# A 5x5 convolution as four 64x64 matmul tiles side by side for eight channels, with its four middle rows on VectorE

## The chip, the cores and the metric

The kernel runs on one NeuronCore of a Trainium2 chip. The metric is the device time of one execution in microseconds, as the median of the runs. In the profile PE is TensorE's matmul, PEld its weight load, DVE is VectorE, ACT is ScalarE, POOL is GpSimd, which also issues most DMAs, and SP is SyncE, which issues the others.

## What is computed

The input is 8 images of 32 channels of 128x128, in float32. Two layers are applied, each of the form x + conv(groupnorm(x)), where the group norm works on groups of two channels.

Layer 0's `conv` is a block-matching filter: for each pixel the eight best of 25 shifted copies are picked by 3x3 patch distance and gathered, and the 256 planes then go through three 1x1 convolutions, each followed by a depthwise 3x3, a product with a DCT of the planes, and an aggregation back to 32 channels. Layer 1's `conv`, which the change is about, is one 5x5 kernel, the same for every channel, with zero padding of 2:

```python
x = x + _L0_conv_ref(_gn(x), ...)
# layer 1: kernel is (5, 5), one for all channels
Xf = X.reshape(B * C, 1, H, W)
out = lax.conv_general_dilated(Xf, kernel[None, None, :, :],
                               window_strides=(1, 1), padding=[(2, 2), (2, 2)], ...)
x = x + out.reshape(B, C, H, W)     # X is _gn(x)
```

## The kernel before

**Steps.** Layer 0 of an image is cut into 17 strips, so there are 8 x 17 = 136 steps (image b, n = 0 to 16), each with four sub-steps i = 3, 2, 1, 0 for the three stages of 1x1 and depthwise convolution and the gathering. The stages lag one another by a step. A step ends, for its strip, with the DCT products (L757 on PE, L760 on DVE) and the aggregation (`pa`, L773 on PE), which is added to the input strip, put into the running statistics and stored to the DRAM buffer `x1d` (L785). For half of the planes the depthwise taps run on DVE as chains of eight `scalar_tensor_tensor` (L688, opened by ACT at L685 and closed by ACT at L692), for the other half on PE in four column tiles of 32 (L709).

**Order.** The orders of PE, DVE and ACT are written out by hand: they are the order of the Python program (`manual_schedule`). The orders of POOL and SP, and with them the DMA queues, are laid out by the framework's scheduler. Side work is written as generators that wait in four queues, "D", "A", "P" and "Q", each item with a cost. At every sub-step `tick` grants the "D" queue a credit, a share of `total`, and the items that fit are emitted there; the other queues are emptied once a sub-step. Side work is `prep(b + 1)`, the patch distances of the next image (differences on DVE at L410, squares on ACT at L418, sums on PE at L425, stores `sq` at L440, window sums on DVE at L474 to L486, sources for the gathering through `xl` and `xtd` at L383 to L395), and `layer1(b)`.

**Layer 1.** `layer1(b)` is pushed when strip 16 of image b has been aggregated. It forms mean and inverse deviation per channel, spreads them to all partitions as `bc` (ACT copy, L806), and then works on four channels at a time, with an image row on each of the 128 partitions: load `xy` from `x1d` (L812), four normalisations of 128x128 into `xm` on DVE (L817), five matmuls of a 128x128 band matrix, one for each dx, into one PSUM bank (L836), the addition to `xy` (L847), and the store (L848). Two `xy` tiles are used in turn, so the load for channels c + 8 follows the store of channels c:

```python
yield "D", 2.1
if c + 4 < C:
    xm = normalise(c + 4)
xy = xys.pop(c)
nc.vector.tensor_add(xy, xy, ps)
nc.gpsimd.dma_start(out[b, c : c + 4].rearrange("c y x -> y c x"), xy)
load(c + 8)
```

The matrix `band[:, dx]` holds the five taps of column dx on its diagonals; it is built once, at the start, on DVE (L329). For images 0 to 6, layer 1 runs as side work in the first steps of the next image; after the last image it runs alone (`until`).

A load of `final_load` for the next strip (`xf`, L744) reads the DRAM buffer `xbd` that the gathering has stored (L608).

Of the kernel before, what the change touches and what calls it, by code (L numbers as in the profile page):

```python
# [9 lines left out]
F32 = mybir.dt.float32  # L10
# [3 lines left out]
ALU = mybir.AluOpType  # L14
ORDERED = {mybir.EngineType.PE, mybir.EngineType.DVE, mybir.EngineType.Activation}

P = 128
C, K, H, W = 32, 8, 128, 128
# [7 lines left out]
HR = 38  # L26
HX = W + 4
SR = 6
# [15 lines left out]
def bm3d_conv_preact(  # L44
# [16 lines left out]
    nc = tc.nc  # L61
    NB = x.shape[0]
# [3 lines left out]
    xnp = ctx.enter_context(tc.tile_pool(name="xn", bufs=1))  # L66
    work = ctx.enter_context(tc.tile_pool(name="work", bufs=2))
# [3 lines left out]
    ps_x = ctx.enter_context(  # L71
        tc.tile_pool(name="ps_x", bufs=5, space=bass.MemoryType.PSUM)
    )
# [49 lines left out]
    band = const.tile([P, 5, P], F32, name="band")  # L123
    kb = const.tile([P, 25], F32, name="kb")
# [22 lines left out]
    with tc.tile_pool(name="setup", bufs=1) as sp, tc.tile_pool(  # L147
        name="setup_ps", bufs=2, space=bass.MemoryType.PSUM
# [22 lines left out]
        for name, w in (("w1", w1), ("w3", w3), ("w5", w5)):  # L171
            t = sp.tile([P, 2, CK], F32, name=f"nat_{name}", tag=f"nat_{name}")
            nc.sync.dma_start(t, w.rearrange("(m p) i a b -> p m (i a b)", p=P))
            if name == "w1":

                nat, t = t, sp.tile([P, 2, CK], F32, name="w1_kc")
# [6 lines left out]
        for name, dst in (("w1", lw1), ("w3", lw3), ("w5", lw5)):  # L183
            for g in range(2):
                ps = spp.tile([P, CK], F32, name=f"ps_{name}_{g}", tag="ps")
                for m in range(2):
                    src = wide[name][:, m, g * P : (g + 1) * P]
# [15 lines left out]
    xtd, xbd, idxd, x1d, stats = {}, {}, {}, {}, {}  # L203
# [12 lines left out]
    def push(task):  # L216
        want = next(task, None)
        if want:
            which, cost, *wait = want
            queues[which].append((cost, task, now[0] + (wait[0] if wait else 0)))  # L220
# [568 lines left out]
    def layer1(b):  # L789

        yield "D", 0.2
        mv = work.tile([P, 2], F32, name=f"mv1_{b}", tag="mv1")
        nc.vector.bn_aggr(mv, stats[b].rearrange("p a b -> p (a b)"))
        mr = yield from group_stats(mv, f"b{b}")
        dg = work.tile([C, 2, C], F32, name=f"dg_{b}", tag="dg")
        for i in range(2):
            nc.vector.tensor_scalar(
                dg[:, i], ident[:C, :C], mr[:C, i : i + 1], None, op0=ALU.mult
            )
        yield "P", 0  # L800
        pb = ps_x.tile([P, 512], F32, name=f"pb_{b}", tag="x")
        nc.tensor.matmul(
            pb[:, : 2 * C], ones, dg.rearrange("p a b -> p (a b)"), start=True, stop=True
        )
        bc = work.tile([P, 2, C], F32, name=f"bc_{b}", tag="bc")
        nc.scalar.copy(bc.rearrange("p a b -> p (a b)"), pb[:, : 2 * C])  # L806
        xys = {}

        def load(c):
            if c < C:  # L810
                xys[c] = work.tile([P, 4, W], F32, name=f"xy_{b}_{c}", tag="xy")
                nc.gpsimd.dma_start(xys[c], x1d[b][c : c + 4].rearrange("c y x -> y c x"))  # L812

        def normalise(c):
            xm = work.tile([P, 4, W], F32, name=f"xm_{b}_{c}", tag="xm")
            for i in range(4):
                nc.vector.tensor_scalar(  # L817
                    xm[:, i],
                    xys[c][:, i],
                    bc[:, 0, c + i : c + i + 1],  # L820
                    bc[:, 1, c + i : c + i + 1],
                    op0=ALU.subtract,
                    op1=ALU.mult,
                )
            return xm

        load(0)
        load(4)
        yield "D", 1.4
        xm = normalise(0)  # L830
        for c in range(0, C, 4):
            yield "P", 0
            ps = ps_x.tile([P, 4, W], F32, name=f"p5_{b}_{c}", tag="x")
            for n, dx in enumerate((0, -2, -1, 1, 2)):
                xa, xz = max(0, -dx), min(W, W - dx)
                nc.tensor.matmul(  # L836
                    ps[:, :, xa:xz],
                    band[:, dx + 2],
                    xm[:, :, xa + dx : xz + dx],
                    start=n == 0,  # L840
                    stop=n == 4,
                )
            yield "D", 2.1
            if c + 4 < C:
                xm = normalise(c + 4)
            xy = xys.pop(c)
            nc.vector.tensor_add(xy, xy, ps)  # L847
            nc.gpsimd.dma_start(out[b, c : c + 4].rearrange("c y x -> y c x"), xy)  # L848
            load(c + 8)

        done.add(b)

    done = set()

# [12 lines left out]
    def unit(stage, u):  # L867
        if 0 <= u < len(units) and units[u]:
            if stage is gather_load:
                at = (units[u][0], units[u][1] % 8 // 2)  # L870
                until(lambda: at in ready, 4.0)
            stage(*units[u])
# [7 lines left out]
        if n == NS:  # L880
            push(layer1(b))

    total = 5.5 + 3.3 + 36 * 1.95 + 4 * 4.6 + 32 * 1.85 + 4 * 2.6 + 8 * 2.1
    owed = [0.0]

    def tick(b, i):
# [6 lines left out]
    def until(cond, credit):  # L893
        while not cond():
            now[0] += 1
            run("D", credit)
            run("A")
            run("P")
            run("Q")

    with tc.manual_schedule(engines=ORDERED):
        push(prep(0))
        push(mixes())
        xbd[0] = dram.tile([P, 2, H, W], F32, name="xbd_0", tag="xbd")
        for i in range(3):
            nc.gpsimd.memset(tb[i][0:64, :, 0], 0.0)
        for u in range(7):
            unit(gather_load, u)
            unit(gather_select, u - 2)
            unit(gather_pixels, u - 3)  # L910
        u = 4

        dt = dv = kept = iter(())

        later = lambda: None

        for s in range(len(steps) + 2):
            if s < len(steps):
                b, n = steps[s]
                if s == 2:  # L920
                    push(bands())
                if n == (0 if b else 4) and b + 1 < NB:
                    until(lambda: b in ready, 4.0)
                    push(prep(b + 1))
                if n == NS - 1 and b + 1 < NB:
                    until(lambda: b + 1 in ready, 4.0)
                    xbd[b + 1] = dram.tile([P, 2, H, W], F32, name=f"xbd_{b+1}", tag="xbd")
            for i in (3, 2, 1, 0):
                si = s - (i - 1 if i else 2)
                live = 0 <= si < len(steps)  # L930
                new_v = new_t = iter(())
                if live:
                    bi, ni = steps[si]

                if live and i:
                    src = source(i, bi, ni)
                    pointwise_v(i, bi, ni, lws[i - 1], src)
                    new_v, new_t = depthwise_v(i, bi, ni), depthwise_t(i, bi, ni)
                    accs[i, bi, ni] = [None, next(new_v)]
                later()  # L940
                later = lambda: None
                if live and not i:
                    if ni == 0:
                        x1d[bi] = dram.tile([C, H, W], F32, name=f"x1d_{bi}", tag="x1d")
                        stats[bi] = work.tile([P, NS + 1, 6], F32, name=f"stat_{bi}", tag="stat")
                    xr, xf, j0, j1 = fins.pop(si)
                run("P")
                if live and not i:
                    final_dct(bi, ni, accs[3, bi, ni], xf, j0, j1)

                run("Q")
                if s < len(steps):
                    unit(gather_select, u + 1)
                    unit(gather_load, u + 3)
                    tick(b, i)
                next(new_v, None)
                if live and i:
                    pointwise_t(i, bi, ni, lws[i - 1], src)
                next(kept, None)
                if not i:  # L960
                    next(dt, None)
                if s < len(steps):
                    unit(gather_pixels, u)
                    u += 1
                if i:
                    next(dt, None)
                run("A")
                next(dv, None)
                next(dt, None)
                kept, dv, dt = dv, new_v, new_t  # L970
                if live and not i:
                    later = partial(end, bi, ni, xr, j0, j1)
                if not i and 0 <= s - 1 < len(steps):
                    fins[s - 1] = final_load(*steps[s - 1])
        next(kept, None)
        later()
        until(lambda: NB - 1 in done, 4.0)


# [60 lines left out]
```

## Time and profile before

| | |
|---|---|
| median of 3 runs | 7144.41 us (7131.88 to 7159.89) |
| the profiled execution | 7131.18 us, its span 7129.4 us |
| granted TensorE clock, mean | 0.978 |
| PE busy | 6700.9 us, 94% of the span, 100226 instructions |
| DVE busy | 5840.1 us, 82% |
| ACT busy | 5061.7 us, 71% |
| POOL busy | 2738.3 us, 38% |
| 5x5 matmuls (L836) | 294.3 us of PE, 640 instructions |
| normalisations (L817) | 74.6 us of DVE, 256 instructions |
| additions (L847) | 43.7 us of DVE, 64 instructions |
| loads (L812), stores (L848) | 49.8 and 50.9 us of POOL, 64 each |

Busy time is summed over the whole span; the span holds 136 steps and the layer 1 of the last image, which begins at about 7056 us and runs with little beside it. One `matmul` of the program is two instructions in the profile here: five matmuls on four channels are ten.

### The profile page before, as it was taken

To read this page: it belongs to the slowest core of one execution; us is meant where nothing else is said; L and a number is where in the kernel's file an instruction comes from. 1 tells how busy PE (TensorE), PEld (TensorE's weight loads), DVE (VectorE), ACT (ScalarE), POOL (GpSimd) and SP (SyncE) were. 2 spreads that over 40 slices of the span, in tenths; PEclk is the share of its full clock that TensorE was granted. 3 is DMA by queue.
4 is the path that set the end of the run, shared out by engine and by line. 5 is a ranking of instruction groups with operands and counts; after the bars stand their busy time and mean duration, and the time that the engine had idled before them with its cause. 6 is when DMAs were issued, how large, how long until landed. Compare 5 with 4: busy or idle time off the path is not lost. (4 is left out here: it accounts for less than half of the span.)

```text
span 7129.4 us, 229485 instructions
## 1 busy us (share of the span) xinstructions
PE 6700.9 (94%) x100226; PEld 3166.8 (44%) x100226; DVE 5840.1 (82%) x8606; ACT 5061.7 (71%) x6706; POOL 2738.3 (38%) x4599
## 2 busy tenths in 40 slices
PE   4699999999999999999999999999999999999997
PEld 1344444444444444444444444444444444444443
DVE  6689978888888898878888898888978889767675
ACT  4687768677686777867677776877768677666762
POOL 6244336333353343533335343543335333232222
PEclk8899999999999999999999999999999999999999
DMA  3566756666565575666656666566656666555652
GB/s 81 130 145 151 155 129 153 142 148 149 134 156 143 138 166 125 160 145 145 154 127 160 141 152 140 142 161 150 152 130 150 151 145 147 125 146 139 149 134 63
DMA packets 765484, 1007.70 MB, mean 141 GB/s; under 512 B 215008, under 2 KB 578592, under 8 KB 764480
## 3 DMA queue, kind: packets, MB, share of 16 engines
q0 software_dynamic: 378400, 733.67, 42.5%
q1 hardware_dynamic: 381056, 256.86, 17.0%
q8 instruction: 788, 12.91, 0.8%
q10 hardware_dynamic: 5024, 2.49, 0.2%
q14 instruction: 216, 1.77, 0.1%
HBM read 542.24 MB, written 217.01 MB: 106 GB/s over the span
## 5 line engine op out<-in xcount | busy, mean ns | idle before, releaser
L688 DVE SCALAR_TENSOR_TENSOR acc<-tv,dwv,acc 128x1024 f32<-128x1024 f32 (+1 forms) x3264 | 4084.0, 1253 | 223.1 <-ACT acc L685 109.5
L709 PE MATMUL pw<-t,dwd 128*32 128x508 f32 (+6 forms) x19584 | 2179.5, 592 | 156.8 <-DMA t<-t 109.4
L709 PEld LDWEIGHTS pw<-t,dwd 128*32 128x32 f32 (+1 forms) x19584 | 702.3, 111 | 1393.8 <-issue 1205.9
L570 POOL DMA_DIRECT2D ib<-idxd x1024 | 575.2, 563 | 1881.5 <-ACT sel L585 1764.8
L584 ACT ACTIVATE ib<-ib,nplace 128x1024 bf16<-128x1024 bf16 x1024 | 1165.4, 1138 | 25.6 <-DMA ib<-idxd 25.6
L585 ACT ACTIVATE sel<-ib 128x1024 f32<-128x1024 bf16 x1024 | 1084.4, 1059 | 32.6
L660 PE MATMUL p<-acc,lw 128*32 128x256 f32 x17408 | 994.1, 375 | 10.3 <-issue 10.0
L637 PE MATMUL pv<-acc,lw 128*128 128x512 f32 (+1 forms) x2112 | 971.9, 602 | 10.5 <-DVE acc L760 6.3
L606 ACT COPY xb<-pg 128x512 f32<-128x512 f32 x512 | 303.6, 593 | 713.5 <-PE pg L599 713.1
L645 ACT COPY tv<-pv 128x512 f32<-128x512 f32 (+2 forms) x784 | 444.8, 584 | 482.0 <-PE pv L637 463.6
L660 PEld LDWEIGHTS p<-acc,lw 128*32 128x32 f32 x17408 | 562.8, 110 | 429.6 <-issue 81.0
L721 ACT ACTIVATE acc<-pw 128x512 f32<-128x512 f32 (+1 forms) x816 | 452.8, 584 | 341.2 <-PE pw L709 340.8
L599 PEld LDWEIGHTS pg<-sel,xt 128*32 128x32 f32 x45056 | 591.2, 111 | 225.7 <-issue 126.1
L599 PE MATMUL pg<-sel,xt 128*32 128x48 f32 x45056 | 593.6, 206 | 82.9 <-issue 53.1
L780 DVE TENSOR_TENSOR xr<-xr,pa 128x256 f32<-128x256 f32 (+2 forms) x136 | 55.1, 405 | 717.9 <-PE pa L773 698.8
L637 PEld LDWEIGHTS pv<-acc,lw 128*128 128x128 f32 x2112 | 381.0, 191 | 407.7 <-issue 376.7
L410 DVE TENSOR_TENSOR df<-xn 128x786 f32<-128x786 f32 (+2 forms) x576 | 529.0, 969 | 17.2 <-PE pd L425 14.6
L667 ACT COPY t<-p 128x512 f32<-128x512 f32 x800 | 423.0, 570 | 119.8 <-PE p L660 116.5
L418 ACT ACTIVATE df<-df 128x786 f32<-128x786 f32 (+2 forms) x576 | 461.1, 862 | 50.4 <-DVE df L410 49.3
L685 ACT ACTIVATE acc<-tv,dwv 128x1024 f32<-128x1024 f32 (+1 forms) x408 | 459.8, 1127 | 45.8 <-PE pa L773 32.1
L637 PE MATMUL pv<-xb,lw 128*128 128x512 f32 x1024 | 475.7, 607 | 0.0
L757 PE MATMUL pc<-xf,ldct 128*128 128x512 f32 (+2 forms) x1056 | 470.9, 588 | 0.0
(128 smaller groups left out, 6397.3 us busy)
## 6 DMA issues: line engine op xcount, KB each, us to landing
ib<-idxd POOLq DMA_DIRECT2D x1024, 256.0 KB
xbd<-xb POOLq DMA_DIRECT2D x128, 1024.0 KB
xf<-xbd POOLq DMA_DIRECT2D x480, 256.0 KB
t<-t SPq DMA_DIRECT2D x792, 128.0 KB, 4.8
t<-t SPq DMA_DIRECT2D x384, 256.0 KB, 4.9
tv<-tv SPq DMA_DIRECT2D x384, 130.0 KB, 4.1
xt<-xtd POOLq DMA_DIRECT2D x240, 176.0 KB
xl<-xs POOLq DMA_DIRECT2D x256, 64.0 KB
```

What stands on the lines that cost most here:

```text
L410: nc.vector.tensor_sub(df[:, :, ca:cz], xn[:, r0 : r0 + SR, ca:cz], xn[:, r0 + dy : r0 + dy + SR, ca + dx : cz + dx],)
L418: nc.scalar.activation(df[:, :, ca:cz], df[:, :, ca:cz], AF.Square)
L570: nc.gpsimd.dma_start(ib.rearrange("p k y x -> p (k y x)"), idxd[b][s4 // 8, s4 % 8, 4 * k0 : 4 * k0 + 8] .rearrange("k x -> (k x)") .part ...
L584: nc.scalar.activation(ib, ib, AF.Square, bias=nplace)
L585: nc.scalar.activation(sel, ib, AF.Relu, scale=-1.0, bias=1.0)
L599: nc.tensor.matmul(pg[C * j : C * (j + 1), :, xa:xz], xt[:, t], sels[j // 2][:, j % 2, :, xa:xz], start=True, stop=True,)
L637: nc.tensor.matmul(ps[:, :hr], lhsT[:, g, P:CK], src(g)[:, h : h + hr], start=g == 0, stop=g == 1,)
L660: nc.tensor.matmul(ps[C * r : C * (r + 1), e, :nb], lhsT[:, g, s], rows[:, r : r + 4 * nb - 3 : 4], start=g == 0, stop=g == 1,)
L685: nc.scalar.activation(acc, rows, AF.Copy, scale=tap)
L688: nc.vector.scalar_tensor_tensor(acc, rows, tap, acc, op0=ALU.mult, op1=ALU.add)
L709: nc.tensor.matmul(pt[u][C * j : C * (j + 1), :, :nb, xa:xz], dwd[0:hi, i - 1, u, j, dx + 1], t[0:hi, j, :, :nb, xa + dx : xz + dx], start ...
L757: nc.tensor.matmul(ps[:, : z - a], ldct[:, m], xf[:, m, a:z], start=True, stop=True)
```

## The change

Layer 1 takes eight channels at a time. For channels c to c + 3 the tile holds the rows in order; for c + 4 to c + 7 a second tile holds the two halves of 64 rows swapped (two loads of 64 partitions), beside a straight copy for the residual. Each of the five dx is then four matmuls of a 64x64 block of the band matrix: rows 0 to 63 and 64 to 127 of the array (r), and output partitions 0 to 63 and 64 to 127 (o), go through the pairs (0, 0), (0, 64), (64, 64), (64, 0), into two PSUM banks. The blocks are the two diagonal blocks of the band matrix, so what rows 0 to 63 give to rows 64 and 65, and the other way round, is left out; the output rows 62 to 65 of this part are not stored (each bank's sum is stored in two parts of 62 rows).

Those four rows come from a new generator, `middle(b, mr)`: four loads put five input rows for each of the four output rows, for all 32 channels, on 4 x 32 partitions, in a tile of the tag `df` that the squares use (four buffers); DVE copies the residual row, normalises the five rows in one operation, and sums the 25 taps with 25 `scalar_tensor_tensor` of 128x128, as 10, 10 and 5 in three "D" items; four stores follow.

An image of layer 1 then has 16 + 4 loads in place of 8 and 16 + 4 stores in place of 8. For images 0 to 6 the loads of the next eight channels are emitted as an "A" item one sub-step after the stores. For the last image all loads are emitted at once, into the buffer of `xn` and into the buffers of `sel`, and the normalisation of the next eight channels stands ahead of the additions. In place of 8 x 2.1, the credit `total` has 4 x 3.6 + 6.6.

```diff
@@ -804,51 +804,123 @@
         )
         bc = work.tile([P, 2, C], F32, name=f"bc_{b}", tag="bc")
         nc.scalar.copy(bc.rearrange("p a b -> p (a b)"), pb[:, : 2 * C])
+        last = b == NB - 1
+        if last:
+            ends = xnp.tile([P, HR, HX], F32, name="ends", tag="xn")
+            ends = ends.rearrange("p r x -> p (r x)")[:, : 8 * 4 * W]
+            ends = ends.rearrange("p (g c x) -> p g c x", g=8, x=W)
         xys = {}
 
         def load(c):
-            if c < C:
-                xys[c] = work.tile([P, 4, W], F32, name=f"xy_{b}_{c}", tag="xy")
-                nc.gpsimd.dma_start(xys[c], x1d[b][c : c + 4].rearrange("c y x -> y c x"))
+            if last:
+                m = work.tile([P, 2, 4, W], F32, name=f"xo_{c}", tag="sel", bufs=4)
+                t = [ends[:, c // 4], ends[:, c // 4 + 1], m[:, 0], m[:, 1]]
+            else:
+                t = [
+                    work.tile([P, 4, W], F32, name=f"{name}_{b}_{c}_{e}", tag=name)
+                    for name, e in (("xy", 0), ("xm", 0), ("xy", 1), ("xm", 1))
+                ]
+            src = x1d[b].rearrange("c y x -> y c x")
+            nc.gpsimd.dma_start(t[0], src[:, c : c + 4])
+            for h in range(2):
+                nc.gpsimd.dma_start(
+                    t[1][64 * h : 64 * h + 64], src[64 - 64 * h : P - 64 * h, c + 4 : c + 8]
+                )
+            nc.gpsimd.dma_start(t[2], src[:, c + 4 : c + 8])
+            xys[c] = t
 
         def normalise(c):
-            xm = work.tile([P, 4, W], F32, name=f"xm_{b}_{c}", tag="xm")
-            for i in range(4):
-                nc.vector.tensor_scalar(
-                    xm[:, i],
-                    xys[c][:, i],
-                    bc[:, 0, c + i : c + i + 1],
-                    bc[:, 1, c + i : c + i + 1],
-                    op0=ALU.subtract,
-                    op1=ALU.mult,
-                )
-            return xm
-
-        load(0)
-        load(4)
-        yield "D", 1.4
-        xm = normalise(0)
-        for c in range(0, C, 4):
+            t = xys[c]
+            for e in range(2):
+                for i in range(4):
+                    nc.vector.tensor_scalar(
+                        t[3 - 2 * e][:, i],
+                        t[e][:, i],
+                        bc[:, 0, c + 4 * e + i : c + 4 * e + i + 1],
+                        bc[:, 1, c + 4 * e + i : c + 4 * e + i + 1],
+                        op0=ALU.subtract,
+                        op1=ALU.mult,
+                    )
+        for c in range(0, C if last else 8, 8):
+            load(c)
+        push(middle(b, mr))
+        for c in range(0, C, 8):
+            if c == 0 or not last:
+                yield "D", 2.0, 1
+                normalise(c)
             yield "P", 0
-            ps = ps_x.tile([P, 4, W], F32, name=f"p5_{b}_{c}", tag="x")
-            for n, dx in enumerate((0, -2, -1, 1, 2)):
+            ps = [
+                ps_x.tile([P, 4, W], F32, name=f"p5_{b}_{c}_{e}", tag="x") for e in range(2)
+            ]
+            t = xys.pop(c)
+            for k, dx in enumerate((0, -2, -1, 1, 2)):
                 xa, xz = max(0, -dx), min(W, W - dx)
-                nc.tensor.matmul(
-                    ps[:, :, xa:xz],
-                    band[:, dx + 2],
-                    xm[:, :, xa + dx : xz + dx],
-                    start=n == 0,
-                    stop=n == 4,
-                )
-            yield "D", 2.1
-            if c + 4 < C:
-                xm = normalise(c + 4)
-            xy = xys.pop(c)
-            nc.vector.tensor_add(xy, xy, ps)
-            nc.gpsimd.dma_start(out[b, c : c + 4].rearrange("c y x -> y c x"), xy)
-            load(c + 8)
-
-        done.add(b)
+                for h in range(2):
+                    for e in range(2):
+                        r, o = 64 * h, 64 * ((h + e) % 2)
+                        nc.tensor.matmul(
+                            ps[e][o : o + 64, :, xa:xz],
+                            band[r : r + 64, dx + 2, r : r + 64],
+                            t[3 - 2 * e][r : r + 64, :, xa + dx : xz + dx],
+                            start=k == 0,
+                            stop=k == 4,
+                        )
+            yield "D", 3.6 if last else 1.6
+            if last and c + 8 < C:
+                normalise(c + 8)
+            for e in range(2):
+                y = t[2 * e]
+                nc.vector.tensor_add(y, y, ps[e])
+                for a, z in ((0, 62), (66, P)):
+                    nc.gpsimd.dma_start(
+                        out[b, c + 4 * e : c + 4 * e + 4, a:z].rearrange("c y x -> y c x"),
+                        y[a:z],
+                    )
+            if c + 8 < C and not last:
+                yield "A", 0, 1
+                load(c + 8)
+        done.add((b, 0))
+    def middle(b, mr):
+        df = work.tile([P, SR, HX], F32, name=f"mid_{b}", tag="df", bufs=4)
+        for r in range(4):
+            nc.gpsimd.dma_start(
+                df[C * r : C * (r + 1), 0:5, 2 : 2 + W], x1d[b][:, 60 + r : 65 + r]
+            )
+        nc.gpsimd.memset(df[:, :, 0:2], 0.0)
+        nc.gpsimd.memset(df[:, :, 2 + W :], 0.0)
+        acc = df[:, 5, 2 : 2 + W]
+        yield "D", 2.6, 1
+        nc.vector.tensor_copy(acc, df[:, 2, 2 : 2 + W])
+        nc.vector.tensor_scalar(
+            df[:, 0:5, 2 : 2 + W],
+            df[:, 0:5, 2 : 2 + W],
+            mr[:, 0:1],
+            mr[:, 1:2],
+            op0=ALU.subtract,
+            op1=ALU.mult,
+        )
+        for dy in range(5):
+            if dy in (2, 4):
+                yield "D", 2.0
+            for dx in range(5):
+                nc.vector.scalar_tensor_tensor(
+                    acc,
+                    df[:, dy, dx : dx + W],
+                    kb[:, 5 * dy + dx : 5 * dy + dx + 1],
+                    acc,
+                    op0=ALU.mult,
+                    op1=ALU.add,
+                )
+        for r in range(4):
+            nc.gpsimd.dma_start(out[b, :, 62 + r], acc[C * r : C * (r + 1)])
+        done.add((b, 1))
 
     done = set()
 
@@ -880,7 +952,7 @@
         if n == NS:
             push(layer1(b))
 
-    total = 5.5 + 3.3 + 36 * 1.95 + 4 * 4.6 + 32 * 1.85 + 4 * 2.6 + 8 * 2.1
+    total = 5.5 + 3.3 + 36 * 1.95 + 4 * 4.6 + 32 * 1.85 + 4 * 2.6 + 4 * 3.6 + 6.6
     owed = [0.0]
 
     def tick(b, i):
@@ -974,7 +1046,7 @@
                     fins[s - 1] = final_load(*steps[s - 1])
         next(kept, None)
         later()
-        until(lambda: NB - 1 in done, 4.0)
+        until(lambda: {(NB - 1, 0), (NB - 1, 1)} <= done, 4.0)
 
 
 # ---- launch: one core; inputs and outputs as the reference has them ----
```

More of the change, by code (lines that the diff above doesn't have):

```diff
@@ L830, in layer1 @@
-        xm = normalise(0)
-        for c in range(0, C, 4):
-            yield "P", 0
-            ps = ps_x.tile([P, 4, W], F32, name=f"p5_{b}_{c}", tag="x")
-            for n, dx in enumerate((0, -2, -1, 1, 2)):
-                xa, xz = max(0, -dx), min(W, W - dx)
-                nc.tensor.matmul(
-                    ps[:, :, xa:xz],
-                    band[:, dx + 2],
-                    xm[:, :, xa + dx : xz + dx],
-                    start=n == 0,
-                    stop=n == 4,
-                )
-            yield "D", 2.1
-            if c + 4 < C:
-                xm = normalise(c + 4)
-            xy = xys.pop(c)
-            nc.vector.tensor_add(xy, xy, ps)
-            nc.gpsimd.dma_start(out[b, c : c + 4].rearrange("c y x -> y c x"), xy)
-            load(c + 8)
@@ new lines, in layer1 @@
+        for c in range(0, C if last else 8, 8):
[5 more added lines that the diff above has]
+                normalise(c)
+            yield "P", 0
+            ps = [
[3 more added lines that the diff above has]
+            for k, dx in enumerate((0, -2, -1, 1, 2)):
+                xa, xz = max(0, -dx), min(W, W - dx)
+                for h in range(2):
[22 more added lines that the diff above has]
+                load(c + 8)
```

## The prediction

> **What bounds the kernel now.** I read the page's totals first, then tables of windows cut at the steps in which layer 1 of an image runs beside layer 0 of the next one, then the timeline of one such step and of the end.
>
> ```profile
> PE 6700.9 (94%) x100226; PEld 3166.8 (44%) x100226; DVE 5840.1 (82%) x8606; ACT 5061.7 (71%) x6706; POOL 2738.3 (38%) x4599
> ```
>
> TensorE is nearly always busy, and VectorE four fifths of the time. The five steps n=0 to 4 after one image boundary (columns: window; its length; busy us of PE, PEld, DVE, ACT, POOL; granted clock; DMA share; GB/s):
>
> ```profile
> 2066.50:2128.20 61.70, 56.77 (x785) 25.69 (x784) 46.97 (x60) 42.16 (x57) 31.08 (x46) 0.94 0.78 169
> 2128.20:2183.90 55.70, 55.70 (x775) 25.78 (x774) 45.75 (x70) 38.51 (x49) 16.40 (x28) 1.00 0.58 145
> 2183.90:2245.30 61.40, 57.81 (x777) 26.78 (x776) 45.63 (x80) 38.52 (x51) 26.41 (x45) 0.97 0.58 138
> 2245.30:2299.20 53.90, 52.47 (x771) 23.89 (x773) 45.55 (x55) 38.34 (x51) 13.35 (x24) 1.00 0.66 140
> 2299.20:2354.90 55.70, 55.70 (x777) 25.80 (x780) 46.65 (x82) 37.64 (x50) 16.05 (x28) 1.00 0.56 144
> ```
>
> Here TensorE sets the time (0 to 5 us idle a step) and VectorE has 8 to 16 us to spare. The convolution's own matmuls, in the same columns cut down to PE and PEld, up to the last image and after it:
>
> ```profile
> 350.00:7050.00 6700.00, 250.78 (x560) 103.48 (x560) 0.99 0.62 144
> 7050.00:7129.40 79.40, 43.53 (x80) 17.55 (x80) 0.83 0.18 54
> ```
>
> So 250.78 / 7 = 35.8 us of TensorE an image where it is hidden, 43.5 us at the end, where it runs alone.
>
> **TensorE's part.** Ten instructions for four channels take 4.42 us (the L836 row below), so eight channels 8.9 us. The change issues 40 for eight channels. If four tiles run at once, that is ten slots of 0.425, 4.4 us: half, 17.8 us saved an image. The nearest row is L709, whose four 128x32 column tiles give 48 instructions in 5.33 us, 0.111 each against 0.442: four at once. At two at once the group is 8.8 us and nothing is saved; one by one, 17 us. I take four at once.
>
> The trace shows column tiles only, never row tiles. [...] Both row tiles here write each of the two banks, on different partitions. [...]
>
> **VectorE's part.** Normalising and adding stay at 256 and 64 instructions. The middle rows add, an image, a copy (like one L817, 0.27 us), a 128x640 scaling (0.6 us, from the L356 row's 2892 ns for 128x5016, and no less than two L817), and 25 of this form, priced by the nearest group:
>
> ```profile
> L329 DVE SCALAR_TENSOR_TENSOR band<-cst,kb,band 128x128 f32<-128x128 f32 x20 | 7.0, 352 | 0.7
> ```
>
> 25 x 0.352 = 8.8, in all 9.7 us in three pieces (4.4, 3.5, 1.8). Inside steps with 8 to 16 us of spare VectorE this costs nothing by itself. What costs is where the first piece stands and when its data come.
>
> **POOL's part, and the new wait.** GpSimd issues 24 more DMAs an image at about 0.8 us each (19 us beside a busy share of 38%; hidden). But order counts. Comparing the two programs' queues: on VectorE the first piece stands where the first normalise (L817) stood, ahead of the eight-operation chains L688 of step n=0. On POOL, for images 0 to 5, the middle rows' four loads stand behind the next image's 18 xtd loads, the xbd store, four xf loads and four x1d stores, just ahead of the sq stores (L440). The timeline of before at that boundary (start, us, engine, line, operation, idle before it and its releaser):
>
> ```profile
> 2070.85 1.49 DVE L817 TENSOR_SCALAR xm<-xy,bc 128x128 f32<-128x128 f32 x4 [0.47 <-ACT bc L806]
> 2072.26 10.52 DVE L688 SCALAR_TENSOR_TENSOR acc<-tv,dwv,acc 128x1024 f32<-128x1024 f32 x8
> 2076.88 4.42 PE L836 MATMUL p<-xm,band 128*128 128x512 f32 x10
> 2087.77 10.52 DVE L688 SCALAR_TENSOR_TENSOR acc<-tv,dwv,acc 128x1024 f32<-128x1024 f32 x8
> 2094.86 2.23 POOL L440 DMA_DIRECT2D sq<-sm  x4 [8.03 <-DMA xf<-xbd]
> 2105.85 10.53 DVE L688 SCALAR_TENSOR_TENSOR acc<-tv,dwv,acc 128x1024 f32<-128x1024 f32 x8 [5.78 <-ACT acc L685]
> 2108.89 5.33 PE L709 MATMUL pw<-t,dwd 96*32 96x512 f32 x48
> 2128.24 1.07 PE L773 MATMUL pa<-acc,lagg 128*32 128x256 f32 x16
> ```
>
> L440 waits until the xf loads have landed, and the loads that take its place wait for the same. So they are issued at 2094.86 to 2097.1; from the end of an issue to the first use an xy load takes 2.3 us in the tail (7071.25 + 0.75 to 7074.34); data at 2099.4. VectorE, in order, stands from 2070.85 until then: 28.6 us. Behind it are queued three chains of L688 (10.5 us each), 5.0 us of window sums between the first two (2082.78 to 2087.77) and the four products L760 (2.5 us, 2116.30 to 2118.8) that the step's last matmul (pa, L773) reads: 2099.4 + 4.4 + 3 x 10.5 + 5.0 + 2.5 = 2142.8 against 2128.24, so +14.6. ScalarE is held at L692 behind the first chain, and TensorE behind ScalarE: its 31.0 us of work between 2097.2 and 2128.24 would end near the same moment, so this bound is as late. The same sum at all six boundaries (first normalise; L440; pa) gives +19.0 (1213.05; 1233.80; 1262.85), +14.6, +19.7 (2933.2; 2955.12; 2983.25), +15.4 (3794.6; 3818.48; 3851.0), +20.6 (4648.6; 4670.95; 4698.29) and +16.3 (5506.7; 5528.58; 5560.18): mean 17.6. It may be 5 more where the engines wait on one another in turn, and, if nothing is caught up, the whole 28; at best the loads land by 2070 and it is nothing.
>
> Against it stands what TensorE gains after that step: 17.8 less what falls into steps n=0 and 1, which leaves 9.2 us in steps n=2 to 5 (22.4 of convolution becomes 13.2); I count 8. Net 17.6 + 0.5 - 8 = +10 a boundary, +60 for six (bounds: -107 with no wait, +135 with a wait of 28 and 6 gained).
>
> At the boundary before the last image the loads stand early in POOL's queue, since no squares follow: no wait, 17.8 less 3 for a less even mix: -15 (-18 to 0).
>
> **The end.** After the last image the convolution runs alone, eight rounds of about 8.2 us:
>
> ```profile
> 7056.39 1.55 POOL L812 DMA_DIRECT2D xy<-x1d  x2 [3.43 <-DMA x1d<-xr]
> 7071.25 0.75 POOL L812 DMA_DIRECT2D xy<-x1d  x1 [2.23 <-DMA out_dram<-xy]
> 7074.34 1.11 DVE L817 TENSOR_SCALAR xm<-xy,bc 128x128 f32<-128x128 f32 x4 [6.37 <-DMA xy<-x1d]
> 7076.34 0.76 POOL L848 DMA_DIRECT2D out_dram<-xy  x1 [4.34 <-DVE xy L847]
> 7122.21 0.76 POOL L848 DMA_DIRECT2D out_dram<-xy  x1 [4.01 <-DVE xy L847]
> ```
>
> A load waits for a store's landing, and VectorE 6.4 us for the load: DMA round trips set this. The change loads all channels up front. Three loads are issued by 7058.7, landed 7061.0, eight normalisations 2.2 to 7063.2; four groups of 4.4 with 1.5 us more for the first, since L836 there starts at 0.85 a pair and falls to 0.43: 7082.3; two additions 1.4, last stores issued by 7087.5, and 6.4 from the last issue to the span's end as now: 7094, -35. If TensorE stays at 0.85 throughout, 7107, -22. VectorE's 9.7 + 8.7 + 5.5 us lie beside. I take -33.
>
> **Sum.** +60 - 15 - 33 = +12. The profiled execution took 7131.18 us (span 7129.4), 13.2 under the median of 7144.41. On its own basis 7143; on the median's, 7144.4 + 11 = 7155. A difference under 0.5% (36 us) a measurement of this kernel can hardly tell from none.
>
> **Rivals.** *No wait:* the loads land before VectorE needs them, or its spare time takes the stall back. For it: 8 to 16 us idle a step. Against it: POOL's order, and L440's wait in this trace. Each boundary then gives between 9.2 and 17.8, say 13.5: -81 - 15 - 33 = -129, 7015 (6990 to 7040). [...]
>
> **How the numbers follow.** Forecast 0.74, no wait 0.16, tiles in turns 0.10. The forecast's own sum runs from -48 (10 less a boundary) to +77 (5 more a boundary, 4 of the 8 not gained, -22 at the end): 0.38 within 36 us, 0.26 above, 0.10 below. With the rivals: faster 0.26, same 0.38, slower 0.36. The range 7030 to 7235 leaves out most of both rivals.
>
> **What would show it.** Right: VectorE idle 25 to 30 us before the first middle-row copy at six boundaries, released by the DMA of the middle rows; a group of 40 matmuls in 4.3 to 4.6 us; step n=0 longer by 15 to 20 us and n=2 to 4 shorter by 2 to 4 each; 35 to 40 us from the last statistics to the end. Wrong: no such idle time (then it is much faster), groups of over 6.5 us (much slower), or idle TensorE in steps n=2 to 5, where I count its gain in full.

## The result, and the profile after

The changed kernel takes 7369.67 us in the median (7351.09 to 7372.95, 4 runs) against 7152.15 of the kernel before on the same chips: a ratio of 1.0306, 95% interval 1.0286 to 1.0326. It is 218 us slower. The forecast was 7155 in a range of 7030 to 7235, so the time lies outside the range, on the slow side.

The profiled execution of the changed kernel has a span of 7349.0 us, 219.6 more than before. Its page begins:

```profile
PE 6642.5 (90%) x100866; PEld 3119.0 (42%) x100866; DVE 5912.9 (80%) x8822; ACT 5058.9 (69%) x6706; POOL 2956.5 (40%) x4807
```

TensorE is busy 58 us less than before and VectorE 73 us more, but the span grew by 220: the engines wait. The table of windows for the steps n=0 to 5 of the same image as in the prediction (same columns; one step more):

```profile
2121.60:2199.30 77.70, 51.13 (x771) 23.67 (x772) 47.52 (x58) 38.25 (x51) 34.14 (x53) 0.82 0.63 138
2199.30:2259.40 60.10, 54.81 (x797) 24.05 (x798) 49.33 (x89) 40.52 (x53) 23.61 (x35) 0.94 0.58 133
2259.40:2314.80 55.40, 52.52 (x805) 24.26 (x804) 45.79 (x70) 39.98 (x52) 21.73 (x32) 1.00 0.58 129
2314.80:2375.60 60.80, 55.43 (x801) 25.03 (x800) 47.74 (x70) 38.42 (x51) 24.15 (x42) 0.94 0.67 162
2375.60:2424.60 49.00, 47.03 (x749) 22.29 (x748) 45.93 (x79) 36.96 (x47) 20.30 (x29) 1.00 0.63 145
2424.60:2485.40 60.80, 54.32 (x795) 23.98 (x794) 45.50 (x70) 38.48 (x52) 22.77 (x33) 0.94 0.66 146
```

Step n=0 is 16.0 us longer than before here (77.7 against 61.7), with TensorE idle for 26.6 us; that is the wait of the prediction. But n=1, 3 and 5 also hold 5.3, 5.4 and 6.5 us of idle TensorE, where before there was 0 to 1.4, and n=2 to 5 were to have become shorter. The timeline of step n=0:

```profile
2134.49 2.50 POOL L744 DMA_DIRECT2D xf<-xbd  x4
2147.19 0.58 POOL L893 DMA_DIRECT2D mid<-x1d  x1 [6.40 <-DMA xf<-xbd]
2152.93 0.23 DVE L900 COPY mid<-mid 128x128 f32<-128x128 f32 x1 [27.34 <-DMA mid<-x1d]
2168.36 1.06 ACT L692 ACTIVATE acc<-acc 128x1024 f32<-128x1024 f32 x1 [25.63 <-DVE acc L688]
2173.50 1.09 PE L491 MATMUL pt<-cst,dsum 128*128 128x128 f32 x4 [25.88 <-ACT acc L685]
```

The chain is as forecast: the loads of the middle rows (L893) are issued when the xf loads have landed, VectorE stands 27.34 us for them (predicted 25 to 30), ScalarE stands at L692 and TensorE behind it. And the tiles do run side by side; one group of 40 in the timeline (step n=3):

```profile
2357.11 4.48 PE L865 MATMUL p<-xm,band 64*64 64x512 f32 x40
```

What the prediction had not priced stands in the groups by line (total, mean ns of one, idle time before them):

```profile
L879 POOL DMA_DIRECT2D out_dram<-xy x112 | 169.9, 1526 | 105.8 <-DVE xy L877 104.2 <-DMA xf<-xbd 1.1 <-issue 0.5
```

A store of 62 rows takes 1.526 us of POOL. Before, a store of 128 rows took half of that:

```profile
L848 POOL DMA_DIRECT2D out_dram<-xy x64 | 50.9, 796 | 170.0 <-DVE xy L847 140.6 <-DVE mx L502 27.6 <-DVE acc L688 1.7
```

In the list of DMA issues of the changed kernel (name, queue, count, size, median us from issue to landing, where the trace holds the landing, here for 12 of them) the same stores need 10.8 us to land:

```profile
out_dram<-xy POOLq DMA_DIRECT2D x112, 124.0 KB, 10.8
```

At the end these stores are the chain that ends last. POOL's timeline after the last image:

```profile
7303.91 3.05 POOL L879 DMA_DIRECT2D out_dram<-ends  x2 [5.09 <-DVE ends L877]
7316.36 1.53 POOL L879 DMA_DIRECT2D out_dram<-ends  x1 [1.13 <-DMA out_dram<-ends]
7329.98 2.99 POOL L879 DMA_DIRECT2D out_dram<-xo  x2
```

and the step of the chain of waits that lies between the first two of them, the landing of a store:

```profile
7305.43 10.09 DMA out_dram<-ends
```

The last addition is over at 7320.2; after it POOL still issues stores until 7333.0, and the span ends 16 us later, not 6.4.

### The profile page after: what moved, and what is told of

Same layout as the page of the kernel before. It is cut to its first block, busy times and chain, and to the rows that moved or that the text cites. A ratio compares the mean times of both kernels' runs of the same rounds, so it can differ in the third digit from the quotient of the medians.

```text
span 7349.0 us, 231279 instructions
## 1 busy us (share of the span) xinstructions
PE 6642.5 (90%) x100866; PEld 3119.0 (42%) x100866; DVE 5912.9 (80%) x8822; ACT 5058.9 (69%) x6706; POOL 2956.5 (40%) x4807
## 5 line engine op out<-in xcount | busy, mean ns | idle before, releaser
L709 PE MATMUL pw<-t,dwd 128*32 128x508 f32 (+6 forms) x19584 | 2229.1, 604 | 229.6 <-DMA t<-t 197.5
L709 PEld LDWEIGHTS pw<-t,dwd 128*32 128x32 f32 (+1 forms) x19584 | 711.1, 113 | 1510.8 <-issue 1327.4
L660 PE MATMUL p<-acc,lw 128*32 128x256 f32 x17408 | 1006.5, 376 | 17.6 <-issue 17.5
L692 ACT ACTIVATE acc<-acc 128x1024 f32<-128x1024 f32 (+1 forms) x408 | 423.0, 1037 | 223.7 <-DVE acc L688 223.4
L410 DVE TENSOR_TENSOR df<-xn 128x786 f32<-128x786 f32 (+2 forms) x576 | 528.8, 967 | 26.7 <-PE pd L425 21.8
L660 PE MATMUL p<-xb,lw 128*32 128x256 f32 x8192 | 477.7, 386 | 0.0
## 6 DMA issues: line engine op xcount, KB each, us to landing
xf<-xbd POOLq DMA_DIRECT2D x480, 256.0 KB, 10.4
```

The lines of the kernel that those rows point to most:

```text
L410: nc.vector.tensor_sub(df[:, :, ca:cz], xn[:, r0 : r0 + SR, ca:cz], xn[:, r0 + dy : r0 + dy + SR, ca + dx : cz + dx],)
L660: nc.tensor.matmul(ps[C * r : C * (r + 1), e, :nb], lhsT[:, g, s], rows[:, r : r + 4 * nb - 3 : 4], start=g == 0, stop=g == 1,)
L709: nc.tensor.matmul(pt[u][C * j : C * (j + 1), :, :nb, xa:xz], dwd[0:hi, i - 1, u, j, dx + 1], t[0:hi, j, :, :nb, xa + dx : xz + dx], start ...
```

## The experiments

Ratios are to the kernel before, with 95% intervals; a time "less than the changed kernel" is the difference of ratios times 7140 us, the level of the kernel before. Steps are timed from one `pa` (L773) to the next, as means over images 1 to 6.

### e1: the middle rows read later

```diff
-        yield "D", 2.6, 1
+        yield "D", 2.6, 4
```

> The changed kernel, but the middle rows' first VectorE item waits four sub-steps and not one, so that it stands behind the three chains of step n=0; where its loads stand in POOL's queue is not moved. If the 27 us of VectorE idle before the middle-row copy are what step n=0 is longer by (20.6 us at six boundaries): that idle is gone, 120 to 165 us less than the changed kernel, 7205 to 7250. If the wait only uncovers another one at the same place (the loads of the next step, the patch sums): within 40 us of the changed kernel.

Measured: 7201.71, ratio 1.0097 (1.0078 to 1.0117): 149 us less than the changed kernel. Step n=0 falls from 77.8 to 59.3 us, and the group of the first copy waits for nothing any more:

```profile
L900 DVE COPY mid<-mid 128x128 f32<-128x128 f32 x8 | 2.1, 263 | 0.0
```

So the wait costs what it seemed to cost, 6 x 18.5 = 111 us in step n=0, and more behind it: in the profiles n=1 to 5 are 65 us shorter over the six images, of which n=6 to 16 give 29 back. With it gone the change is still slower than the kernel before. The loads' place in POOL's queue was not moved; it was enough to read them three sub-steps later.

### e2: whole stores

```diff
-                for a, z in ((0, 62), (66, P)):
-                    nc.gpsimd.dma_start(out[b, c + 4 * e : c + 4 * e + 4, a:z]..., y[a:z])
+                nc.gpsimd.dma_start(out[b, c + 4 * e : c + 4 * e + 4]..., y)
...
-        for r in range(4):
-            nc.gpsimd.dma_start(out[b, :, 62 + r], acc[C * r : C * (r + 1)])
```

> The changed kernel, but each sum is stored in one transfer of 128 rows and the middle rows are not stored (rows 62 to 65 of the output hold incomplete sums); their arithmetic stays. If the 62-row stores (1.52 us of POOL each and about 11 us to land, against 0.80 before) cost time by holding up the DMAs behind them: 60 to 100 us less than the changed kernel, 7270 to 7310, of which 20 at the end. If they lie beside other work: 20 us less, all of it at the end.

Measured: 7185.48, ratio 1.0070 (1.0053 to 1.0087): 168 us less than the changed kernel, more than expected. The wait is still there (164.2 us before the copy, in all). What goes is the idle TensorE of the steps behind: n=1, 3 and 5 are shorter by 7.3, 6.9 and 8.2 us than in the changed kernel, and the end by 25.1. A whole store lands after 3.6 us.

The table of waits tells whom TensorE waited for there: the t rows, which transfers issued by SyncE move and which L709 reads. First the changed kernel, then e2 (total us, times, longest):

```profile
PE pw L709 <- DMA t<-t: 197.5, 64, 12.4
PE pw L709 <- DMA t<-t: 88.5, 40, 12.5
```

Before it was 109.4 us. In n=1 to 5 of images 1 to 6 alone it is 99.7 us in the changed kernel and 2.8 in e2. In the changed kernel a transfer of t rows that is issued in the 5 us after the issue of a sum's store begins lands after 10.4 us in the median (60 transfers), all others after 4.9; in e2 it is 5.9 (42 transfers) and 4.7. So beside a store of 62 rows the transfers of another engine landed late, and TensorE waited for them.

### e3: half of the convolution left out of the kernel before

```diff
-            for n, dx in enumerate((0, -2, -1, 1, 2)):
+            taps = (0, -2) if c % 8 else (0, -2, -1)
+            for n, dx in enumerate(taps):
```

> The kernel before with half of the 5x5 matmuls left out (three or two of five dx, in turn); all orders as before. It takes 17.9 us of TensorE from each of seven boundaries and about 22 from the end. If TensorE's time in these steps is worth its full price: 7 x 17.9 + 5 = 130 us less than before, 7020. If the matmuls only cover the time in which the t rows are moved (VectorE and ScalarE set the pace once they are gone): 20 to 60 less, 7090 to 7130, with TensorE idle in front of L709 where the matmuls were.

Measured: 7024.83, ratio 0.9830 (0.9812 to 0.9848): 121 us less than before. The steps n=0 to 7 lose 15.5 us an image, of 17.9 us of matmuls taken out. TensorE's time in these steps is worth nearly its full price, and the rival (that the matmuls merely cover the moving of the t rows) is out.

### e4, e5, e6 and e10: what makes a store dear

```diff
-            nc.gpsimd.dma_start(out[b, c : c + 4].rearrange("c y x -> y c x"), xy)
+            for a, z in ((0, 62), (66, P)):          # e5: (0, 60), (68, P)
+                nc.gpsimd.dma_start(out[b, c : c + 4, a:z].rearrange("c y x -> y c x"), xy[a:z])
```

> The kernel before with each store cut in two of 62 rows (rows 62 to 65 are not stored). If such stores are dear by themselves: 40 to 100 us more than before, 7190 to 7250, with loads and gathers on POOL waiting for them, and at the end at least 8 x 2 us more. If POOL has room for them: within 25 us of before.

> The kernel before with each store cut in two of 60 rows (rows 60 to 67 are not stored): as many transfers as in the run with two of 62 rows, which took 147 us more than before. If it is the count of 62 x 4 = 248 rows of 512 B, which does not go into 16 engines evenly, that makes a store dear (240 does): about 0.6 us of POOL an issue, 3 to 4 us to land, within 25 us of before. If it is the doubled number of stores: again 1.5 us an issue or 100 us and more over before.

Measured: with 62 rows 7282.18, ratio 1.0199 (1.0182 to 1.0216), 142 us more than before; in the profile the end alone takes 52.5 us more. With 60 rows 7141.18, ratio 1.0008 (0.9994 to 1.0021): no difference. As many transfers, and nothing else in the kernel was touched. The groups of the stores, first with 62 rows, then with 60, and the landing of those of 60 from the list of issues:

```profile
L849 POOL DMA_DIRECT2D out_dram<-xy x128 | 195.5, 1531 | 171.9 <-DVE xy L847 118.0 <-DVE mx L502 37.5 <-issue 16.1
```

```profile
L849 POOL DMA_DIRECT2D out_dram<-xy x128 | 86.7, 681 | 178.5 <-DVE xy L847 147.5 <-DVE mx L502 28.9 <-issue 1.9
```

```profile
out_dram<-xy POOLq DMA_DIRECT2D x128, 120.0 KB, 3.3
```

My reason for the 60 was that 248 rows of 512 bytes do not divide among 16 engines and 240 do. The next run puts eight channels into a store, 496 rows, which would divide; it also has the later read of e1:

```diff
+                y = work.tile([P, 8, W], F32, name=f"xy_{b}_{c}", tag="xy", bufs=1)
+                t = [y[:, 0:4], m[0], y[:, 4:8], m[1], y]
...
+            for a, z in ((0, 62), (66, P)):
+                nc.gpsimd.dma_start(out[b, c : c + 8, a:z].rearrange("c y x -> y c x"), t[4][a:z])
```

> The changed kernel with the later read of the middle rows, and with the two sums of eight channels in one tile, so that one store carries 62 rows of eight channels (496 rows of 512 B, 31 for each of 16 engines) and eight stores an image replace sixteen; the output is whole. If the wait and the 62-row stores are the two things that make the change slow, and the rest of its sum holds: 150 and 168 us less than the changed kernel, 7030 to 7070, faster than before by 1 to 1.5%. If the two prices overlap (both end in the same TensorE idle): 7100 to 7150. If such a store is as dear as four channels' were: 7150 to 7200.

Measured: 7263.42, ratio 1.0179 (1.0152 to 1.0207), above e1 and above all that was expected. Such a store takes 2.06 us of POOL and 17.1 us to land. There are half as many, so that POOL spends 115.0 us on those of images 0 to 6 where the changed kernel spends 169.9; what makes e6 slow is then not POOL's own time.

```profile
L879 POOL DMA_DIRECT2D out_dram<-xy x56 | 115.0, 2057 | 87.5 <-DVE xy L877 70.5 <-DVE acc L688 10.6 <-issue 5.9
```

So it is not the total of rows. Left is the number of partitions, 62. (With whole stores the one tile for eight channels costs nothing: e9 below has it too.) The next kernel is the one before with another number in each image:

```diff
+            rows = (64, 63, 62, 61, 56, 52, 48, 32)[b]
+            for a, z in ((0, rows), (P - rows, P)):
```

> The kernel before with every store cut in two parts of 64, 63, 62, 61, 56, 52, 48 or 32 rows, another count for each of the eight images (rows between the parts are not stored). If a row count that is no multiple of 4 is what makes a store dear: about 1.5 us an issue and 9 us or more to land for 63, 62 and 61, and 0.5 to 0.7 us and 3 to 4 us for the others. If only some counts are dear: by image, as measured.

The stores of each image, from the groups in a window around its convolution, for 64, 63, 62, 61, 56, 52, 48 and 32 rows in turn (total us and mean ns behind the first bar; one execution, whose whole time is not used):

```profile
L850 POOL DMA_DIRECT2D out_dram<-xy x14 | 9.1, 654 | 18.9 <-DVE xy L847 14.7 <-DVE mx L502 4.1
L850 POOL DMA_DIRECT2D out_dram<-xy x14 | 10.9, 786 | 21.4 <-DVE xy L847 17.0 <-DVE mx L502 4.3
L850 POOL DMA_DIRECT2D out_dram<-xy x14 | 21.4, 1533 | 14.3 <-DVE xy L847 11.5 <-DVE mx L502 2.6 <-issue 0.2
L850 POOL DMA_DIRECT2D out_dram<-xy x14 | 34.7, 2484 | 12.8 <-DVE xy L847 9.6 <-DVE mx L502 1.9 <-DVE df L410 0.8
L850 POOL DMA_DIRECT2D out_dram<-xy x14 | 9.6, 693 | 21.7 <-DVE xy L847 16.6 <-DVE mx L502 5.1
L850 POOL DMA_DIRECT2D out_dram<-xy x14 | 9.7, 694 | 18.6 <-DVE xy L847 14.3 <-DVE mx L502 4.3
L850 POOL DMA_DIRECT2D out_dram<-xy x13 | 7.8, 602 | 4.8 <-DVE xy L847 4.8
L850 POOL DMA_DIRECT2D out_dram<-xy x16 | 8.8, 552 | 41.4 <-DVE xy L847 41.4
```

0.65, 0.79, 1.53, 2.48, 0.69, 0.69, 0.60 and 0.55 us. "No multiple of 4" is not the rule either: 63 is cheap. For these nine counts the order is that of the largest divisor of the row count that is not above 16: 16, 9, 2, 1, 14, 13, 16, 16 (and 15 for the 60 of e5, at 0.68). Any bound from 16 to 19 gives the same numbers; the profile counts 16 DMA engines. The issue times grow as this number falls, from 0.55 to 0.69 us at 13 to 16 to 2.48 at one; a whole store of 128 rows, with 16 and twice the rows, takes 0.80.

The packets in the traces go with this order. A partition gives a store 4 x 512 = 2048 bytes, and the whole stores go out in packets of 4096 alone: at the end of the kernel before the trace has none of 2048, at the end of the changed kernel 32 for 16 stores of 62 rows. Around the stores of 63, 62 and 61 rows (from 2 us before the first to 20 us behind the last) GpSimd's queue has 784, 672 and 656 packets of 2048 bytes, and around the same images' stores in the kernel before 640: 144, 32 and 16 more, which is 9, 2 and 1 for each of the 16 stores. My estimate from these counts is that a store went out in so many pieces of 7, 31 and 61 partitions, each with half a packet left over; the pieces themselves are in no trace. At the end of e4, while the two stores of 62 rows are alone on the queue, never more than six of their packets overlap, and for all but 0.1 us of it at most four; at the end of e5 15 do, of a whole store, in the kernel before, up to 18. So the packets of a store of 62 rows went out a few at a time, and those of 60 and of 128 rows many at once.

For the landing the comparison is e4 against e5, 9.1 us (17 landings in the trace) against 3.3 (63). e10 gives only one to three an image, and they do not sort the counts as was expected: 9.2 us for 64 rows, 7.7 for 63, 9.0 and 9.9 for 62, 13.0 to 15.2 for 61, 7.2 for 56, 7.5 for 52, 2.2 to 7.0 for 48, 1.9 for 32.

### e7: early loads at the end, alone

```diff
+            ends = ends.rearrange("p (g c x) -> p g c x", g=8, x=W)     # in the buffer of xn
...
-        load(0)
-        load(4)
+        for c in range(0, C if last else 8, 4):
+            load(c)
```

> The kernel before, with all loads of the last image's convolution issued up front into the buffer of xn; nothing else is changed. If the end is set by the round trip of store and load: eight rounds of 8.2 us become eight of 4.5 at most, 25 to 30 us less than before, 7105 to 7112. If by something else there (the colder clock, the additions): within 10 us of before.

Measured: 7120.09, ratio 0.9967 (0.9953 to 0.9982): 24 us less, and in the profile the stage from the last `pa` to the end takes 55.6 us and not 80.2, 24.6 less. The end was bound by the round trips.

### e8 and e11: both causes removed, then the middle rows too

```diff
 e8 = e1 + e2
 e11:
-        push(middle(b, mr))
-    total = ... + 4 * 3.6 + 6.6
+    total = ... + 4 * 3.6
```

> The changed kernel with the later read and with whole stores of 128 rows and no stores of the middle rows (rows 62 to 65 hold incomplete sums). If the two prices add: 7370 - 150 - 168, 7040 to 7070. If they overlap: 7100 to 7150.

> Later read and whole stores as in the run that took 7083, and the middle rows left out altogether (their loads, their 27 VectorE operations and their share of the credit). If VectorE's 9.7 us an image lie in its spare time: within 20 us of 7083. If the steps have no room for them: 60 to 90 us less, 6995 to 7020.

Measured: e8 7082.71, ratio 0.9921 (0.9902 to 0.9940); e11 7084.58, ratio 0.9933 (0.9910 to 0.9955). The two prices nearly add: 275 of 149 + 168 = 317 us. They overlap in n=1 to 5, which e1 shortens by 65 us over the six images, e2 by 149 and both by 173. Leaving out the middle rows, 9.8 us of VectorE an image, gains nothing. That they cost nothing is not shown by it: the smaller credit also moves the squares of the next image (to 4, 6, 4, 4, 4, 8, 4, 2 in n=0 to 7; 4, 4, 6, 4, 4, 5, 7, 2 in e8), and e13 below shows that this alone can cost more than the 60 to 90 us that were at stake.

### e9: the whole computation with whole stores

```diff
-            for a, z in ((0, 62), (66, P)):
-                nc.gpsimd.dma_start(out[b, c : c + 8, a:z]..., t[4][a:z])
+            nc.gpsimd.dma_start(out[b, c : c + 8].rearrange("c y x -> y c x"), t[4])
...
+    def middle_store(b):                  # called when both parts of image b are done
+        if {(b, 0), (b, 1)} <= done:
+            for r in range(4):
+                nc.gpsimd.dma_start(out[b, :, 62 + r], maccs[b][C * r : C * (r + 1)])
```

(from e6; the middle rows' sums have a small tile of their own, `maccs[b]`, that lives until then.)

> The whole computation: later read of the middle rows, eight channels' sums stored by one transfer of 128 rows, and the middle rows stored over them once the last of these has landed. If the dear stores and the wait are all that separates the change from its gain: as the run with whole stores and no stores of the middle rows, 7083, or up to 15 us above it, 0.992 to 0.995 of before. If one load of eight channels behind each store takes the gain back: at or above before.

Measured: 7082.20, ratio 0.9921 (0.9901 to 0.9940). This version computes everything and beats both kernels, by 0.8% and 3.7%. In its profile the gain over the kernel before lies in image 7 (18 us) and at the end (30); images 1 to 6 take 3 us more than before. The price of the later stores of the middle rows is POOL's wait for the whole store under them, 43.2 us over the eight images; e8, which has none of these stores, takes as long:

```profile
L878 POOL DMA_DIRECT2D out_dram<-xy x28 | 26.2, 934 | 64.2 <-DVE xy L877 64.2
L926 POOL DMA_DIRECT2D out_dram<-macc x32 | 16.3, 515 | 50.4 <-DMA out_dram<-xy 43.2 <-issue 3.6 <-DMA out_dram<-ends 3.6
```

### e12 and e13: where the side work falls

Half of the matmuls left out gained 15.5 us an image in e3; e9 gains 9.7 in the steps n=0 to 5, and then gives 2.8 and 3.3 back in n=6 and 7, and some more later, which is why images 1 to 6 gain nothing. Only the credit is changed:

```diff
-    total = ... + 4 * 3.6 + 6.6
+    total = ... + 4 * 3.6 + 6.6 + 4       # e13: - 8
```

> The whole computation as in the run that took 7082 (later read, whole stores, the middle rows stored over them), with the credit of the side work raised by 4 (192), so that the squares of the next image are spread over the steps n=0 to 7 as 6, 4, 4, 4, 4, 6, 4, 4 and not as 4, 4, 6, 4, 4, 6, 6, 2. If steps n=6 and 7 give the gain back because the squares run out early and the matmuls then wait: 20 to 60 us less, 7020 to 7060. If the order of the side work does not matter: within 15 us of 7082.

> As before, with the credit lowered by 8 (180): squares 4, 2, 6, 6, 2, 6, 6, 4. If the order of the side work is what gives the gain back: another time than 7082 by 20 us or more, either way, with the loss in the steps with six squares. If it does not matter: within 15 us of 7082.

Measured: e12 7112.43, ratio 0.9964 (0.9951 to 0.9978), 31 us more than e9; e13 7180.98, ratio 1.0060 (1.0041 to 1.0078), 99 us more. The differences (L410) between two `pa` tell where the squares fall: in e9 as expected, in e13 too but for small shifts in later images, but in e12 as 6, 2, 6, 4, 4, 6, 4, 4. Where a step has six and not four, it is longer than in e9: n=0 of e12 by 8.1 us, n=3 of e13 by 6.2. Step n=7, with four and not two, is shorter by 5.1 and 4.2. But n=6 with four and not six is no shorter (0.9 longer, e12), and in e13 n=8 and n=9, almost without squares, are longer by 6.9 and 5.8. So the place of the side work is worth as much as the whole change. "Squares that run out early" fits what is lost in n=7; what gives the gain back in n=6 and behind n=7 stays open.

## Why the prediction was wrong

The stages of the three profiles, in us against the kernel before (from its 7129.4; the stages are cut at `pa`):

| stage | predicted | changed kernel | e2, whole stores |
|---|---|---|---|
| n=0 of images 1 to 6 | +109 | +124 | +126 |
| n=1 to 5 of images 1 to 6 | -48 | +93 | -56 |
| n=6 to 16 of images 1 to 6 | 0 | +21 | +37 |
| image 7 up to its last strip | -15 | -7 | -14 |
| the end | -33 | -14 | -39 |
| all, with image 0 | +12 | +220 | +51 |

**Right: the wait.** Place, releaser and size were as forecast: 27.2 us of idle VectorE in the mean of the six boundaries, each step n=0 longer by 20.6 us against 17.6 + 0.5. e1 removed it and gained 149 us, more than these 6 x 20.6, because n=1 to 5 became shorter too.

**Right: four tiles at once.** 40 instructions in 4.48 us, inside the forecast's 4.3 to 4.6. In the group shown above the first four start within 20 ns of one another and each runs for 640 ns, two of them in each bank. Both row tiles write both banks, on different partitions, and they did not take turns. No run shows tiles taking turns, which have 0.10 in the prediction and a part of its 0.36 for slower: two at a time would have made this a group of 8.8 us, twice the 4.42 of ten instructions before, and 4.48 were measured.

**Right up to n=5, for image 7 and for the end, once the stores are cheap.** -9.3 a boundary in n=1 to 5 against -8, -14 for image 7 against -15, -39 at the end against -33 (e2). That the middle rows' arithmetic is free was not tested by itself (e11).

**Wrong: the step "POOL's part".** It priced "24 more DMAs an image at about 0.8 us each (19 us beside a busy share of 38%; hidden)". It took the row of a store of 128 rows for one of 62. A store of 62 rows took 1.53 us to issue and 10.8 to land. POOL's share is not 19 but (2956.5 - 2738.3) / 8 = 27 us an image, 16 x 1.52 + 4 x 0.51 - 8 x 0.80 = 20 of it for the stores alone. And it was not hidden: beside these stores the t rows landed after 10.4 us where others took 4.9, and TensorE waited 99.7 us for them in n=1 to 5 of images 1 to 6, in e2 2.8; and at the end POOL still issues stores when the last addition is over. Alone, in the kernel before, such stores cost 142 us (e4); in the changed kernel their absence is worth 168 (e2). The prediction gave both ends for each unknown cost but for this one, which it did not take for unknown; no rival was built on it. With 168 on top of the forecast's 7155 the sum would have been 7323. Of the prediction's own signs of being wrong, idle TensorE in n=2 to 5 is the one that came.

**Not counted:** +37 us in the steps n=6 to 16 (e2), for which the sum has 0. With both causes removed it is +60 (e8) and takes back most of what n=1 to 5 gain, 80 us. In e3, which leaves the order as it was, these steps are 12 us longer, and in e12, where only the credit differs from e9, 7 longer and not 61 (but n=0 takes 48 more); that points to the place of the side work, but how it costs this time stays open.

## What to carry to other kernels

The price of a store went here with its shape and not only with its bytes: 1.53 us of POOL for 62 rows, 0.68 for 60, 0.80 for 128. Before a tile that GpSimd stores is cut by rows, measure a store of that count, or write the whole tile and then the few rows over it (e9, 0.9921 of before). Before an addition is called hidden on a queue with room, find the row of the trace with the same shape, and if there is none, give it a range. A wait at the first read of a late load was taken away by reading later (e1, 149 us less) as well as, at the end, by loading earlier (e7, 24 us less), and a change of one number is enough to see which.

## What the runs showed of the hardware that was not expected

Issue time on POOL for a store of n partitions x 4 x 512 bytes: 0.55 us for 32, 0.65 for 64, 0.68 for 60, 0.79 for 63, 1.53 for 62, 2.48 for 61 (e4, e5, e10); to land, 3.3 us for 60 and 9.1 for 62 in kernels otherwise equal. Beyond the packets of whole stores, one of 2048 bytes a store for 61, two for 62, nine for 63. Two more rows, 3% more bytes, took the store from nothing to 2% of a 7 ms kernel.

Four 64x64 tiles in two banks, each bank written by both row tiles on different partitions, ran 40 instructions in 4.48 us, 0.112 each, as fast as four column tiles of 32 (0.111).

The slow stores went with late transfers of another engine: t rows whose transfers SyncE issued landed after 10.4 us behind a store of 62 rows and after 5.9 behind a whole one (e2).
